# Layer 3 of a four-layer network on one core: the window permutation moves from PE's reads and ACT's eviction to PE's PSUM writes

## The chip, the cores and the metric

The kernel runs on one core of a Trainium2 chip. The metric is the device time of one execution in microseconds (us). One execution was also taken by the hardware profiler; the tables and lines below are from it. PE is TensorE, DVE is VectorE, ACT is ScalarE, POOL is GpSimd, and SP is the engine that issues the DMAs.

## The reference, cut to what matters

Eight images of 32 channels and 256 x 256 pixels pass four layers, each of the form `x = x + layer(groupnorm(x))`. Layer 0 is a depthwise 5 x 5 convolution behind a 1 x 1 one, layer 1 an "adder" convolution (a sum of absolute differences over 32 x 9 taps for each of 32 outputs), layer 2 a 3 x 3 convolution. Layer 3, which the change touches, works on windows of 8 x 8 pixels:

```python
wins = xh.reshape(B, H // WS, WS, W // WS, WS, C).transpose(0, 1, 3, 2, 4, 5).reshape(-1, WS, WS, C)
y = _layernorm(wins, pn_g, pn_b)
a = _fastkan(...)                 # along the rows of a window
d = _fastkan(...)                 # along its columns
e = _fastkan(y.reshape(b, WS * WS, C), ...)
z = a + d + e
z = _fastkan(z.reshape(b, WS * WS, C), ...)
out = z + wins
```

A `_fastkan` is a layer norm, eight Gaussian bases `exp(-((ln - grid) / denom)**2)`, a product with weights over features and bases, and the product of `silu(x)` with a second weight matrix. There are four of them; below they are KAN 0 to 3, and KAN 3 is the last, whose output is added to its window's input.

## The kernel before, in words

**Tiles.** A tile of layer 3 (a "unit") is [128, 2048] fp32: four blocks of 32 channels on the partitions, eight rows of 256 pixels along the free axis. An image has `U` = 8 units, so there are 64 in all. Within 512 columns (two rows) pixels lie in image order, `(r v j)`: row, window, column in the window. KAN 2 and KAN 3 work in the order `(r j v)`, the window index innermost. Whoever reads image order in window order steps 8 elements (32 bytes) from one element to the next.

**Products.** `mm16` (line 587) does one 32-wide channel product of a whole unit: 16 fp32 matmuls of 32 x 32 x 512, four row blocks by four column blocks of PE's array, into the four banks of the PSUM tile psB (`psB` is a single buffer, [128, 4, 512]). The trace has two MATMUL rows for each fp32 matmul, so an `mm16` is 32 rows, all at line 593. Who called it is seen from the tiles: `bas,tl` and `arena,tl` are bases, centrings and sums with constant weights, `si,tl` the SiLU terms, `arena,wt` the centred input of `front`, `si,wt` the residual of KAN 3.

**Layer 3, unit by unit.** `front` (line 1278) loads the unit's input x3 and centres it over the channels with `cenf`, reading it through `windows` (line 1200), so that PSUM holds window order; ACT copies it out (line 1219), squares it (line 1224), PE sums the squares (line 1232), and ACT makes the inverse roots. `middle` scales it (line 1272, on DVE). `kan(n, t)` (line 1334) scales its input and makes eight bases: a square on ACT (line 1368) or on DVE (line 1374), the exponential on ACT (line 1381), and for each basis one `mm16` accumulating into psB (`main`, line 1354). Then the SiLU term (line 1434) and what is in `more`: for KAN 2 the outputs of KANs 0 and 1, for KAN 3 the residual, x3 read once more through `windows` (line 1432). ACT evicts psB to SBUF: KANs 0 to 2 in order (line 1447), KAN 3 back to image order (line 1449):

```python
nc.scalar.activation(
    sb(o).rearrange("p (i v j) -> p i j v", i=8, j=8),
    psB.rearrange("p s (r j v) -> p (s r) j v", r=2, j=8),
    AF.Identity,
    bias=obias,
)
```

It reads PSUM in order and writes SBUF 8 elements apart. SP then stores the unit to the output (line 1471). For the last image, where layer 1 no longer runs, `variance` and `scale` work in two halves on psA instead of psB (`parts`, line 1204).

**Layer 1.** DVE makes a distance of 128 x 4128 bf16 (line 977; some halves on ACT, line 979) and PE sums it with eight matmuls, a "gather" (`gather`, line 990, trace line 999), into psA. There are three buffers for distances (`NDV`, kind "dv").

**What sets the order.** All of it is ordered ahead by a list planner (`Plan`, line 105). Each task has an engine, a planned duration (`mm16` 1.03 us, an eviction 1.97, a gather 0.53) and a rank; `Plan.run` plays the four queues SP, PE, DVE and ACT against each other with these durations and a latency from one engine to the next (`LAT`, line 110), and each engine's instructions are then written out in the order that results. Distances and gathers are "fillers" (`Plan.fill`, line 346, and `Pass.on_pe`, line 404) that go in where an engine has no ranked task. A square may go to DVE (`square.other`) if DVE is free when ACT isn't. Ranks are the number of the image plus a share: layer 3 of image b has b + 1.1 to b + 1.98, so the highest is below 8.1 + 0.88.

Of the kernel before, what the change touches and what calls it, by code (L numbers as in the profile page):

```python
# [20 lines left out]
C = 32  # L21
# [7 lines left out]
FS = F // S  # L29
GRID = 8  # L30
# [35 lines left out]

BASE = 16 * (W + 2) // 2
ROOM = [("bas", 3 * BASE, BASE), ("si", 3 * F, F), ("rs", F // 2, F // 4), ("xr", F // 2, F // 2), ("sb", 10 * F, 0)]
URGENT = 2
IDLE = 8.0  # L70
NDV = 3
# [33 lines left out]
class Plan:  # L105
# [1 line left out]

    LAT = {"PE": 0.15, "DVE": 0.12, "ACT": 0.25, "SP": 2.0}  # L110

    def __init__(self, room):
        self.tasks, self.passes = [], []

        self.free, self.places, at = {}, {"psA": [0], "psB": [0], "psV": [0, 1], "dv": list(range(NDV))}, 0
        for kind, n, size in room:
            if size:
                self.places[kind] = list(range(n // size))
            else:
                self.free[kind] = [(at, n)]  # L120
                at += n
        self.first_pass = 0
        self.sets = []

    def add(self, eng, us, fn, r=(), w=(), rank=0.0, after=(), table=None, spare=0, kb=0, acc=()):
# [102 lines left out]
    def run(self):  # L228
# [23 lines left out]
        while left or any(not p.done for p in self.passes):  # L252
            moved = True
            while moved:
                moved = False
                for e in engines:
                    if busy[e] > now + 1e-9:
                        continue
                    best = self.fill(e, True)
                    if best is None:  # L260
                        for t in ready[e]:
                            if best is not None and (t.rank, t.n) >= (best.rank, best.n):
                                continue
                            if t.table in (LN_EXP, SILU) and t.stretch != self.head:
                                continue
                            if t.eng != e and not all(p.done for p in self.passes[self.first_pass :]):
                                continue
                            if t.gate and not t.gate(self):
                                continue
                            if self.fits(t.need, t.spare):  # L270
                                best = t
                        if best is not None:
                            ready[best.eng].remove(best)
                            if best.other:
                                ready[best.other[0]].remove(best)
                                if best.eng != e:
                                    self.sets[best.stretch][1] -= 1
                                    best.eng, best.us, best.fn, best.table = (*best.other, None)
                    if best is None:
                        best = self.fill(e, False)  # L280
                    if best is None:
                        continue
                    t = best
                    self.take(t.need)
                    us = t.us
                    t.load = None
                    if t.table in (LN_EXP, SILU):
                        self.sets[self.head][1] -= 1
                        self.head += not self.sets[self.head][1]
                        if table != t.table:  # L290
                            t.load = table = t.table
                            us += 1.4
                    t.start = now
                    order.append(t)
                    if e == "SP":
                        busy[e] = now + us
                        mover = max(mover, now + us) + t.kb / 210.0
                        t.end = mover
                    else:
                        busy[e] = t.end = now + us  # L300
                        if e == "ACT" and t.n is not None:
                            self.idle = t.end
                    heapq.heappush(events, (busy[e], 1, count, None))
                    heapq.heappush(events, (t.end, 2, count, t))
                    count += 1
                    moved = True
            if not events:
                break
            now = self.now = events[0][0]
            while events and events[0][0] <= now + 1e-9:  # L310
                _, what, _, t = heapq.heappop(events)
                if what == 0:
                    arrive(t)
                elif what == 2:
                    t.over = True
                    left -= t.n is not None
                    for b in t.bufs:
                        b.left -= 1
                        if not b.left:
                            self.drop(b)  # L320
                    for d in t.outs:
                        d.wait -= 1
                        lat = 0.0 if d.eng == t.eng and t.eng != "SP" else self.LAT[t.eng]
                        d.ready = max(d.ready, t.end + lat)
                        if not d.wait:
                            if d.ready <= now:
                                arrive(d)
                            else:
                                push(d)
                    if t.n is None:  # L330
                        t.ended(t)
# [10 lines left out]

    def slack(self, p):
        return p.b == 0 or self.now - self.idle > IDLE

    def fill(self, e, urgent):

# [17 lines left out]
class Pass:  # L365
# [38 lines left out]
    def on_pe(self, plan, urgent):  # L404
# [3 lines left out]

        late = (9 - len(self.sums)) * 9 < 9 * 9 - self.left or not (self.terms or self.rest or self.queue)
        if self.sums and len(self.queue) < URGENT and (late or not (urgent or self.queue)):  # L410
            t, us, bufs, n = self.sums.pop(0), 0.53, [], 1
            fn = lambda: self.parts.gather(self, None, None, t)
        elif self.queue and (len(self.queue) >= URGENT or not urgent):
            o, t, d = self.queue.pop(0)
            us, bufs, n = 0.53, [d], 1
            fn = lambda: self.parts.gather(self, d, o, t)
        elif not self.added and self.residual.over and (self.left < 20 or not urgent):
            us, bufs, n = 1.75, [], 0
            fn = lambda: self.parts.residual(self)
            self.added = True  # L420
        else:
            return None
# [14 lines left out]
def kernel(  # L437
# [146 lines left out]
        for q in range(NQ):  # L584
            fn(slice(q * C, (q + 1) * C), q)

    def mm16(o, weights, src, start, stop, first=0):

        for j in range(S):
            for i in range(first, min(4, first + o.shape[1])):  # L590
                rows = slice(i * C, (i + 1) * C)
                w_ = weights(i, j) if callable(weights) else weights[rows]
                nc.tensor.matmul(o[j * C : (j + 1) * C, i - first, :], w_, src(rows, i, j), start=start, stop=stop)  # L593

    def spans(t):
        return lambda rows, i, j: t[rows, j * FS : (j + 1) * FS]
# [573 lines left out]
    def stage3(b, norm, x3buf, rank, span):  # L1170
# [5 lines left out]
        def fold():  # L1176
# [20 lines left out]
        stat = {(k, t): (Buf("psV"), Buf("rs")) for t in range(-2, U + 2) for k in "ABC"}  # L1197
        turn = lambda t: r((t + 2) / (U + 4))
        st = [dict() for _ in range(U)]
        windows = lambda t: (  # L1200
            lambda rows, i, j: t[rows, j * FS : (j + 1) * FS].rearrange("c (r v w) -> c r w v", r=2, w=8)
        )

        def parts():

            if b < nb - 1:
# [71 lines left out]
        def front(t, after, rk):  # L1278
# [2 lines left out]
                "SP", 0.5, lambda: nc.sync.dma_start(sb(xt), im["x3"][t]),  # L1281
                r=[x3buf[t]], w=[xt], rank=rk, after=[*norm.done.writers, *after], spare=SPARE + F, kb=1024,
            )
            cen = lambda o, i: mm16(o, cenf, windows(sb(xt)), True, True, i)
            st[t]["c4"] = variance(4, ("A", t - 1), cen, cb, rk, [xt, sm["cenf"], sm["c3"]], xt)

        def middle(t):
# [46 lines left out]
        def kan(n, t, at, rk):  # L1334
# [13 lines left out]
                        nc.sync.dma_start(dst, to_f(d)[g])  # L1348

            acc = Buf("psB")  # L1350
            bases = []
            exps = []

            def main(k):
                mains.append(plan.add(
                    "PE", 1.03,
                    lambda bas=bases[k]: mm16(psB, tl[:, WK + 9 * n + k, :], spans(sb(bas)), k == 0, False),
                    r=[bases[k]], w=[acc], rank=rk,
                ))
                if k == 0:  # L1360
# [65 lines left out]
            if n == 3:  # L1426
# [2 lines left out]
                    "SP", 0.5, lambda a=a: nc.sync.dma_start(sb(a), im["x3"][t]),  # L1429
                    r=[x3buf[t]], w=[a], rank=rk, after=exps[4:5], spare=F, kb=1024,  # L1430
                )
                more.append((a, resf, lambda rows, i, j, a=a: windows(sb(a))(rows, i, j)))
            plan.add(
                "PE", 1.03, lambda: mm16(psB, tl[:, WK + 9 * n + GRID, :], src, False, not more),
                r=[si], w=[acc], rank=rk,
            )
            for m, (a, wm, s_) in enumerate(more):
# [5 lines left out]
            obias = b4 if n == 3 else col(KCOL + 2 * n + 1)  # L1443

            def evict():
                if n < 3:
                    nc.scalar.activation(sb(o), psB.rearrange("p s f -> p (s f)"), AF.Identity, bias=obias)  # L1447
                else:
                    nc.scalar.activation(  # L1449
                        sb(o).rearrange("p (i v j) -> p i j v", i=8, j=8),  # L1450
                        psB.rearrange("p s (r j v) -> p (s r) j v", r=2, j=8),
                        AF.Identity,
                        bias=obias,
                    )

            st[t][f"end{n}"] = plan.add(
                "ACT", 1.97, evict, r=[acc] + ([sm["c3"]] if n == 3 else []), w=[o], rank=rk - 0.001
# [216 lines left out]
```

## Time and profile before

| | us |
|---|---|
| median of 3 runs | 15973.13 |
| lowest, highest | 15972.10, 15999.17 |
| the profiled execution | 15969.78 |
| its span, first to last instruction | 15967.3 |

| engine | busy us | share of the span |
|---|---|---|
| DVE | 13454.6 | 84% |
| PE | 12928.0 | 81% |
| ACT | 12386.4 | 78% |
| PE weight loads (overlap PE) | 4325.8 | 27% |

The span has three parts: up to 2.4 ms the first image goes through layers 0 and 1; up to 14.6 ms layer 1 of one image runs beside layer 3 of the image before and the other layers between them; from 14.6 ms the last image's layers 2 and 3 run alone.

How to read a group of the profile: line, engine, operation, output <- inputs, shapes, x count | busy us, mean ns of one | idle us of the engine just before them, and what ended it. In a timeline a row is start, duration, engine, line, operation and count of merged instructions, with the engine's idle time before it in brackets. In a table of stretches, each engine has its busy us and, in brackets, its instructions; the last three numbers are the granted clock, the DMA share and GB/s.

### The profile page before, as it was taken

The page shows a single profiled execution, that of the slowest core. Times are in us where ns is not written, and L with a number is a line of the kernel's source. Part 1 is how long each engine was busy: PE and PEld are TensorE (multiplying, and loading weights), DVE is VectorE, ACT ScalarE, POOL GpSimd, SP SyncE. Part 2 cuts the span into 40 slices and gives each one's busy share as a digit, 9 for nine tenths or more (in the row PEclk, how much of TensorE's full clock was granted, in tenths as well). Part 3 has the DMA queues.
Part 4 walks back from the last instruction along what each step waited for, and adds up shares of the span by engine and source line. Part 5 has one row for each costly group of instructions (what it writes and reads, how often), then busy time and mean ns, then how long its engine had stood idle before and what let it go on. Part 6 is the DMA issues. An engine that isn't in the chain of part 4 may idle for free. (4 is left out here: it accounts for less than half of the span.)

```text
span 15967.3 us, 560619 instructions
## 1 busy us (share of the span) xinstructions
PE 12928.0 (81%) x260296; PEld 4325.8 (27%) x260296; DVE 13454.6 (84%) x12544; ACT 12386.4 (78%) x6843; POOL 16.7 (0%) x25
## 2 busy tenths in 40 slices
PE   5889887987887888788887888788878888877666
PEld 4333322222332222232222222222222222222222
DVE  2889889898878889888999988999898989897465
ACT  0899749678658766866888987899779987997687
POOL 0000000000000000000000000000000000000000
PEclk8989899999999999899999999899999999998777
DMA  4332446445445444643554454444544454444554
GB/s 117 78 96 54 105 113 169 109 107 153 130 101 152 126 112 120 166 106 105 152 132 123 126 134 122 122 123 127 127 126 126 126 122 138 116 132 114 144 154 130
DMA packets 1192870, 1970.85 MB, mean 123 GB/s; under 512 B 362752, under 2 KB 878848, under 8 KB 1092224
## 3 DMA queue, kind: packets, MB, share of 16 engines
q1 hardware_dynamic: 1190528, 1934.98, 46.1%
q8 instruction: 2036, 33.36, 0.9%
q14 instruction: 306, 2.51, 0.1%
HBM read 1162.83 MB, written 771.75 MB: 121 GB/s over the span
## 5 line engine op out<-in xcount | busy, mean ns | idle before, releaser
L977 DVE TENSOR_SCALAR dv<-qh,w1q 128x4128 bf16<-128x4128 bf16 (+1 forms) x8831 | 10521.9, 1248 | 1376.3 <-PE psA L999 1319.3
L999 PE MATMUL psA<-dv,sel_b 128*32 128x512 bf16 x71240 | 5434.0, 405 | 1339.6 <-DVE dv L977 1054.2
L999 PEld LDWEIGHTS <-sel_b 128*32 128x32 bf16 x82944 | 2053.9, 97 | 6792.6 <-issue 5786.5
L1368 ACT ACTIVATE bas<-arena,kb 128x2048 f32<-128x2048 f32 x1386 | 2762.3, 1993 | 408.3 <-DVE arena L1272 262.9
L1381 ACT ACTIVATE bas<-bas 128x2048 f32<-128x2048 f32 x1386 | 2653.1, 1914 | 39.0
L979 ACT ACTIVATE dv<-qh,w1n 128x2064 bf16<-128x2064 bf16 x827 | 1628.6, 2009 | 1126.8 <-PE psA L999 1035.3
L593 PE MATMUL psB<-bas,tl 32*32 32x512 f32 x48416 | 1955.5, 652 | 491.1 <-ACT bas L1381 247.6
L873 PE MATMUL psB<-arena,wt 32*32 32x512 f32 (+1 forms) x51040 | 1848.5, 607 | 99.5 <-issue 61.4
L593 PE MATMUL psB<-arena,tl 32*32 32x512 f32 x22496 | 909.4, 621 | 161.7 <-ACT si L1449 46.1
L593 PEld LDWEIGHTS psB<-bas,tl 32*32 32x32 f32 x48416 | 535.2, 107 | 1384.3 <-ACT bas L1381 518.8
L873 PEld LDWEIGHTS psB<-arena,wt 32*32 32x32 f32 x51040 | 651.2, 104 | 778.1 <-issue 607.1
L1368 ACT ACTIVATE arena<-arena,kb 128x2048 f32<-128x2048 f32 x410 | 816.1, 1991 | 0.0
L1381 ACT ACTIVATE arena<-arena 128x2048 f32<-128x2048 f32 x410 | 785.0, 1915 | 12.3
L624 DVE BATCH_NORM_STATS2 tiny<-arena 128x6 f32<-128x512 f32 x768 | 473.5, 679 | 351.8 <-ACT arena L906 246.0
L999 PE MATMUL psA<-qh,sel_b 128*32 128x512 bf16 x9216 | 672.2, 393 | 92.3 <-DMA qh<-q 77.9
L1447 ACT ACTIVATE si<-psB,cols_sb 128x2048 f32<-128x2048 f32 x192 | 377.4, 1966 | 453.3 <-PE psB L593 369.9
L1272 DVE TENSOR_TENSOR arena<-psB,arena 128x2048 f32<-128x2048 f32 x280 | 640.5, 2287 | 86.2 <-PE psB L1264 79.2
L593 PE MATMUL psB<-si,tl 32*32 32x512 f32 x14080 | 630.6, 624 | 48.8 <-ACT si L1447 19.5
L1129 PE MATMUL psB<-arena,tl 32*32 32x512 f32 (+3 forms) x16384 | 626.6, 608 | 14.7 <-issue 14.4
L1224 ACT ACTIVATE arena<-arena 128x2048 f32<-128x2048 f32 x320 | 612.7, 1915 | 15.7 <-DMA x<-arena 5.8
L1264 PE MATMUL psB<-rs,tl 32*32 32x512 f32 x8960 | 338.9, 630 | 222.5 <-DVE arena L1272 128.2
L906 ACT ACTIVATE arena<-psB,cc 128x2048 f32<-128x2048 f32 x64 | 125.7, 1964 | 493.2 <-PE psB L894 493.2
(151 smaller groups left out, 7686.6 us busy)
## 6 DMA issues: line engine op xcount, KB each, us to landing
arena<-x SPq DMA_DIRECT2D x128, 1024.0 KB
arena<-y SPq DMA_DIRECT2D x128, 1024.0 KB
si<-sy SPq DMA_DIRECT2D x512, 256.0 KB
arena<-in_x_dram SPq DMA_DIRECT2D x240, 384.0 KB
arena<-in_x_dram SPq DMA_DIRECT2D x256, 256.0 KB
x<-arena SPq DMA_DIRECT2D x256, 256.0 KB
xr<-x SPq DMA_DIRECT2D x512, 128.0 KB
x<-xr SPq DMA_DIRECT2D x512, 128.0 KB
```

Of the source, the lines that this page charges most:

```text
L593: nc.tensor.matmul(o[j * C : (j + 1) * C, i - first, :], w_, src(rows, i, j), start=start, stop=stop)
L624: nc.vector.bn_stats(self.stats[:, at + i, :], a[:, i * 512 : (i + 1) * 512])
L873: nc.tensor.matmul(o[:, lo - 2 * j : hi - 2 * j, c0:c1], wt[rows, t, :], d[rows, lo + dy + 2 : hi + dy + 2, c0 + dx : c1 + dx], start=firs ...
L977: nc.vector.tensor_scalar(dst, src, w1q[:, at : at + 1], 0.0, ALU.subtract, ALU.max)
L979: nc.scalar.activation(dst, src, AF.Relu, bias=w1n[:, at : at + 1])
L999: nc.tensor.matmul(psA[j * C : (j + 1) * C, i, :], sel_b[:, n, :], src[:, at : at + 2, t % 3 : t % 3 + W], **flags,)
L1129: nc.tensor.matmul(o[:, lo - 2 * j : hi - 2 * j, c0:c1], (wc if t == 4 else tl[:, W2T + t, :])[rows], d[rows, lo + dy + 1 : hi + dy + 1, c ...
L1224: plan.add("ACT", 1.9, lambda: nc.scalar.activation(sb(sq), sb(c), AF.Square), r=[c], w=[sq], rank=rk)
L1272: lambda ps=ps, at=at: nc.vector.tensor_tensor(sb(c)[:, at], ps().rearrange("p s f -> p (s f)"), sb(c)[:, at], ALU.mult),
L1368: lambda k=k, bas=bas: nc.scalar.activation(sb(bas), sb(rb), AF.Square, bias=kb[:, n, k : k + 1]),
L1381: lambda k=k, bas=bas, square=square: nc.scalar.activation(sb(bas), sb(bas), AF.Exp, scale=-1.0, bias=0.0 if square.eng == "ACT" else kbsq ...
L1447: nc.scalar.activation(sb(o), psB.rearrange("p s f -> p (s f)"), AF.Identity, bias=obias)
```

## The change

Two views are added and handed to `mm16`, which can now write its PSUM rows in another order than it reads. In `front` the centring reads x3 in order and writes it to PSUM in window order (`to_window`: 32 elements apart). In KAN 3 all ten products (eight bases, SiLU term, residual) go to PSUM in image order (`by_window`: the first nine read window order and write 8 elements apart; the residual reads and writes in order). KAN 3's eviction then is that of the other KANs. `windows` goes.

The planner also changes: the latencies, the gather's planned duration (0.53 to 0.49), 0.05 us planned for PE at each switch between gathers and ranked work, and a branch (`AHEAD`) that lets a filler go ahead of a PE task whose rank is more than 9 above the number of the image that layer 1 is at.

```diff
+AHEAD = 9.0
...
-    LAT = {"PE": 0.15, "DVE": 0.12, "ACT": 0.25, "SP": 2.0}
+    LAT = {"PE": 0.2, "DVE": 0.15, "ACT": 0.3, "SP": 2.0}
...
-        self.first_pass = 0
+        self.first_pass, self.filling = 0, False
...
-                        if best is not None:
+                        if best is not None and e == "PE" and best.rank > self.image() + AHEAD:
+                            piece = self.fill(e, False)
+                            if piece is not None:
+                                best = piece
+                        if best is not None and best.n is not None:
                             ready[best.eng].remove(best)
...
                     t.load = None
+                    if e == "PE":
+                        us += 0.05 * ((t.n is None) != self.filling)
+                        self.filling = t.n is None
...
+    def image(self):
+        return next((p.b for p in self.passes[self.first_pass :] if not p.done), len(self.passes))
...
-            t, us, bufs, n = self.sums.pop(0), 0.53, [], 1
+            t, us, bufs, n = self.sums.pop(0), 0.49, [], 1
...
-            us, bufs, n = 0.53, [d], 1
+            us, bufs, n = 0.49, [d], 1
...
-    def mm16(o, weights, src, start, stop, first=0):
+    def by_window(o):
+
+        return o.rearrange("p (r v j) -> p r j v", r=2, j=8)
+
+    def to_window(o):
+
+        return o.rearrange("p (r j v) -> p r v j", r=2, j=8)
+
+    def mm16(o, weights, src, start, stop, first=0, view=lambda o: o):
...
-                nc.tensor.matmul(o[j * C : (j + 1) * C, i - first, :], w_, src(rows, i, j), start=start, stop=stop)
+                nc.tensor.matmul(view(o[j * C : (j + 1) * C, i - first, :]), w_, src(rows, i, j), start=start, stop=stop)
...
-        windows = lambda t: (
-            lambda rows, i, j: t[rows, j * FS : (j + 1) * FS].rearrange("c (r v w) -> c r w v", r=2, w=8)
-        )
...
-            cen = lambda o, i: mm16(o, cenf, windows(sb(xt)), True, True, i)
+            cen = lambda o, i: mm16(o, cenf, spans(sb(xt)), True, True, i, to_window)
...
+            view = by_window if n == 3 else lambda o: o
...
-                    lambda bas=bases[k]: mm16(psB, tl[:, WK + 9 * n + k, :], spans(sb(bas)), k == 0, False),
+                    lambda bas=bases[k]: mm16(psB, tl[:, WK + 9 * n + k, :], spans(sb(bas)), k == 0, False, view=view),
...
-                more.append((a, resf, lambda rows, i, j, a=a: windows(sb(a))(rows, i, j)))
+                more.append((a, resf, lambda rows, i, j, a=a: sb(a)[rows, j * FS : (j + 1) * FS]))
             plan.add(
-                "PE", 1.03, lambda: mm16(psB, tl[:, WK + 9 * n + GRID, :], src, False, not more),
+                "PE", 1.03, lambda: mm16(psB, tl[:, WK + 9 * n + GRID, :], src, False, not more, view=view),
...
             def evict():
-                if n < 3:
-                    nc.scalar.activation(sb(o), psB.rearrange("p s f -> p (s f)"), AF.Identity, bias=obias)
-                else:
-                    nc.scalar.activation(
-                        sb(o).rearrange("p (i v j) -> p i j v", i=8, j=8),
-                        psB.rearrange("p s (r j v) -> p (s r) j v", r=2, j=8),
-                        AF.Identity,
-                        bias=obias,
-                    )
+                nc.scalar.activation(sb(o), psB.rearrange("p s f -> p (s f)"), AF.Identity, bias=obias)
```

## The prediction

> **What bounds the kernel now.** I read the busy times first, then the same shares by stretches of the span, because the stages have different limits.
>
> ```profile
> PE 12928.0 (81%) x260296; PEld 4325.8 (27%) x260296; DVE 13454.6 (84%) x12544; ACT 12386.4 (78%) x6843; POOL 16.7 (0%) x25
> ...
> 8000.00:14000.00 6000.00, 4890.53 (x92432) 1534.18 (x92421) 5436.81 (x4614) 5166.62 (x2865) 8.56 (x7) 0.93 0.48 127
> 15098.00:15868.00 770.00, 519.44 (x9576) 185.16 (x9576) 477.78 (x241) 636.81 (x386) 0.00 (x0) 0.77 0.54 147
> ```
>
> Over the whole span no engine is above 84%. In the middle (8 to 14 ms: one image's adder passes beside the KAN units of the image before), VectorE (DVE) is busy 5436.8 of 6000 us, 91%, ScalarE (ACT) 86%, TensorE (PE) 82%. There the three take turns at being late: the waits put 1319 us of DVE's idle time to PE's gather line 999 and 1054 us of PE's to DVE's line 977. In the tail (from 14.6 ms, the last image's eight units with no adder left) ACT is the fullest, 637 of 770 us, 83%. The chain that ended last lies in the tail alone, and its largest single line is the `mm16` helper, L593, with 1.3% of the span.
>
> The groups, shapes kept apart, price what is touched:
>
> ```profile
> L593 PE MATMUL psB<-bas,tl 32*32 32x512 f32 x48416 | 1955.5, 652 | 491.1 <-ACT bas L1381 247.6 <-ACT arena L1219 64.1 <-ACT si L1447 63.9
> ...
> L1447 ACT ACTIVATE si<-psB,cols_sb 128x2048 f32<-128x2048 f32 x192 | 377.4, 1966 | 453.3 <-PE psB L593 369.9 <-PE psA L999 70.0 <-DMA arena<-in_x_dram 9.1
> ...
> L1449 ACT ACTIVATE si<-psB,cc 128x2048 f32<-128x2048 f32 x64 | 262.0, 4094 | 107.5 <-PE psB L593 107.4
> ...
> L593 PE MATMUL psB<-si,wt 32*32 32x512 f32 x2048 | 153.8, 1085 | 4.2 <-issue 4.0
> ...
> L593 PE MATMUL psB<-arena,wt 32*32 32x512 f32 x1792 | 117.6, 1086 | 10.4 <-ACT arena L1219 6.1 <-DVE cc L1190 3.2 <-ACT si L1447 0.9
> ```
>
> The last KAN's eviction (L1449) moves the same 128x2048 as the other KANs' (L1447) and takes 4094 ns against 1966: it writes SBUF 32 bytes apart. The two products that read windows, the residual (`si,wt`) and the centred input (`arena,wt`), take 1085 ns a row against some 620 for rows that read in order. One `mm16` is 32 rows (16 fp32 products, two rows each). How one eviction sits in time, in the middle:
>
> ```profile
> 10583.23 2.50 DVE L977 TENSOR_SCALAR dv<-qh,w1q 128x4128 bf16<-128x4128 bf16 x2 [1.40 <-PE psA L999]
> ...
> 10583.54 2.10 PE L593 MATMUL psB<-si,wt 32*32 32x512 f32 x32
> ...
> 10585.57 0.62 PE L999 MATMUL psA<-dv,sel_b 128*32 128x512 bf16 x8
> ...
> 10585.82 4.15 ACT L1449 ACTIVATE si<-psB,cc 128x2048 f32<-128x2048 f32 x1 [1.63 <-PE psB L593]
> 10586.01 1.03 PE L1232 MATMUL psV<-arena,tl 128*32 128x512 f32 x8
> 10586.24 6.33 DVE L977 TENSOR_SCALAR dv<-qh,w1q 128x4128 bf16<-128x4128 bf16 x5 [0.51 <-PE psA L999]
> ```
>
> The residual occupies PE for 2.03 us before the next gather; DVE, out of buffers, idles 1.40 and 0.51 us around it, and ACT idles 1.63 us for the residual before its 4.15 us eviction. PE waits little here, as gathers fill it; over all units it idles about 83 us behind L1449.
>
> **The change, part by part.**
>
> *Eviction.* 64 units (8 images of 8) x (4.094 - 1.966) = 136 us off ACT. Both of its sides are in order now, as in L1447, so I count this as nearly certain.
>
> *Residual and centred reads.* An `mm16` that reads windows spans 2.10 us from first start to last end, one in order 1.15. Residual: it reads and writes in order now, as psB holds image order; 64 x 0.95 = 61 us of PE. Centred input (reads in order, writes permuted): 56 units on psB x 0.95 = 53 us; the last image's 8 units go in 16 halves on psA, where the rows fall from 1089 ns to about 750: 16 x 0.34 = 5 us. Together 119 us of PE, 58 of them only if the permuted write is free.
>
> *Permuted writes.* They replace the read in the 64 centred products and are new in nine of each last KAN (eight bases and the SiLU term): 64 x 9 = 576 `mm16`. They land 32 bytes apart (centred input: 128), and no row of this trace writes PSUM so at length, so I bound it. It can't gain, since the writes it replaces are in order. From above, the nearest rows are the reads 32 bytes apart: +0.95 us each, 547 us of PE, and then the centred products' 58 us aren't saved either. I take zero, for this reason:
>
> ```profile
> 2615.61 1.04 PE L999 MATMUL psA<-qh,sel_b 128*32 128x512 bf16 x16
> ...
> 2616.48 0.61 PE L999 MATMUL psA<-dv,sel_b 128*32 128x512 bf16 x8
> ...
> 2617.02 1.14 PE L593 MATMUL psB<-bas,tl 32*32 32x512 f32 x32
> ...
> 2617.90 1.47 PE L593 MATMUL psB<-si,tl 32*32 32x512 f32 x32
> ```
>
> At full clock 16 bf16 gathers take 1.04 us and 8 take 0.61, so eight more cost 0.43; they put 2 x 512 columns into each column tile, 0.215 us per 512 columns of a bank. The fp32 `mm16` from 2617.02 to the next at 2617.90 takes 0.88 us for 2 x 512 columns into each of four banks that fill side by side: 0.44 us per 512. So fp32 products write a bank at half the rate that the gathers show it to take. What the strided accesses here cost is a factor of two (the read 2.10 for 1.15 us, ACT's write 4.09 for 1.97); a write that is halved from the rate of the gathers still keeps up with fp32.
>
> [...]
>
> *The planner's constants.* The order of every queue (PE, DVE, ACT, SP) is made by the plan, so latencies of 0.2/0.15/0.3, a gather at 0.49 in place of 0.53, and 0.05 at each switch between gathers and other PE work reorder everything, the DMA issues among it. The same work is issued (no DMA or wait is added), though the plan also chooses whether a square or a distance runs on ACT or on DVE, so busy time can move between the two. 82944 gather rows are 10368 gathers: -0.04 each is 415 us less planned on PE, and the switches put up to 0.05 x 10368 = 518 back. The isolated gather of the trace (0.61) and the next one's 0.43 lie on both sides of either figure, so no row says which order is better. I take zero, with 100 us either way: some 8% of the 1319 us that DVE waits for gathers. The `AHEAD` branch asks for a rank over the image's number plus 9; the highest rank is below 8.1 + 0.88 = 8.98, and the lowest image is 0, so it never runs and costs nothing.
>
> *What passes on.* Per unit the residual, then the eviction, then the next user of the single psB form one chain; 0.95 + 2.13 = 3.08 us leave it. In the tail I count all of it: 8 x 3.08 = 25 us. In the middle the fullest engine is DVE. I took DVE's busy share in slices of 2 us around the 54 residuals between 2.4 and 14.6 ms: it falls from about 0.92 to 0.80, 0.82, 0.61, 0.92, 0.83, 0.82, which is 0.72 x 2 = 1.4 us lost per unit, while around the other KANs' evictions it stays at 0.92. So if DVE binds, 56 x 1.4 = 80 us come back; if ACT binds, 56 x 3.08 = 172. With 91% against 86% both bind by turns; I take the middle, 126. Around the centred products DVE shows no lasting dip (0.86 to 1.00), so I count their 58 us at nothing: gathers and waiting distances hide them, and uncovered they'd be 58 more. SP's store of the output (L1471) is issued 2 to 3 us earlier and nothing waits on that. Sum: 126 + 25 = 151 us off the profiled execution's 15969.8 us (its span 15967.3 and 2.5 around it), 15819. The median of the runs shown is 15973.1, 3 us more and less than a measurement tells; I say **15820**. What is late next is ACT's square and exp of the bases (2.0 + 1.9 us each).
>
> **Rivals.**
>
> *The strided write costs what the strided read costs: slower.* +547 us of PE. Cover: where ACT makes a base in 3.9 us, PE's base (1.15) and three gathers (some 1.5) leave over 1 us, and 0.95 would hide; where bases stand ready (the first three or four of a unit) or DVE has no buffer, nothing hides it. At half, +274, less the 151 of eviction and residual: +123, **16090**; if all passes, 547 - 151 gives 16370. It decides from where the loss on 576 products at half weight eats the 151 us: 151 / (0.5 x 576) = 0.52 us per `mm16`. For: reads and ACT's writes both lose a factor of two at this stride. Against: the gathers' rate.
>
> *Hidden or eaten.* DVE binds, the 80 us are all that returns, and the new order costs 50 to 100: within 0.2% (32 us), about **15960**. For: 91% DVE, and a DVE wait is as much its own order as PE's.
>
> *A worse order alone.* The direct gain is real and the order costs 200 or more: **16020**. Against: the eviction and the strided reads were planned at 1.97 and 1.03, which they now meet, so the plan fits better than before.
>
> **The numbers.** Forecast, 15690 to 15930: 0.70. Strided write: 0.17. Hidden: 0.08. Worse order: 0.05. A measurement here tells about 0.2% from no change, so faster 0.70, same 0.08, slower 0.22. Range for 8 in 10: below, 151 + 100 (order) + 58 (centred products uncovered) gives 15660; above, it goes into the strided write's case to 16100, leaving out half of that case (0.09) and, at both ends, up to 0.1 elsewhere.
>
> **What would show it.** The 64 evictions that use `cc` fall from 4.09 to 1.97 us; `si,wt` and `arena,wt` rows fall to 610 to 650 ns and their `mm16` to 1.15 us; the mean of the rows of bases (`bas,tl`) stays at some 650. If the write costs, 18432 of the rows from bases and SiLU stand near 1085 and PE's busy time grows by some 500 us. DVE's share around the last KAN's eviction should rise by 1.4 us per unit; ACT's busy time falls by 136 us, give or take what the plan moves to or from DVE. I am wrong if the strided write loses over 0.52 us, or if PE's waits for DVE and ACT grow elsewhere by more than 100 us through the order.

## The result and the profile after

The changed kernel takes 15815.5 us (median, 15803.4 to 15820.4) against 15973.7 for the kernel before: ratio 0.9895, 95% interval 0.988 to 0.991, 158 us less. In a later session, beside experiment 11, it took 15790.9 where the kernel before took 15978.9: ratio 0.988 (0.9865 to 0.9895), 188 us less. The predicted time was 15820. In the changed kernel `mm16` is line 612, the gather 1018, the distance 996, the centred eviction 1234 and every KAN's eviction 1462.

The page's busy times:

```profile
PE 12814.9 (81%) x260296; PEld 4330.4 (27%) x260296; DVE 13427.1 (85%) x12536; ACT 12262.5 (78%) x6849; POOL 33.1 (0%) x25
```

The middle stretch and 770 us of the tail (columns as in the section on the profile before):

```profile
8000.00:14000.00 6000.00, 4883.39 (x93994) 1566.43 (x93994) 5529.40 (x4715) 5199.70 (x2919) 11.63 (x7) 0.94 0.49 130
14940.00:15710.00 770.00, 527.00 (x9706) 179.48 (x9701) 482.90 (x245) 631.80 (x389) 0.00 (x0) 0.76 0.55 151
```

Against before PE is busy 113 us less and ACT 124; DVE's share of the middle goes from 91% to 92%, and counted from 2.4 to 14.4 ms its idle time falls from 1331 to 1237 us. The tail looks as before, with ACT the fullest.

The groups by shape, in the changed kernel (the last row belongs to the last image's halves; in the kernel before it had a mean of 1089 ns):

```profile
L612 PE MATMUL psB<-bas,tl 32*32 32x512 f32 x48544 | 1953.2, 653 | 438.8 <-ACT bas L1397 240.1 <-DVE arena L1287 59.5 <-ACT arena L1234 52.6
...
L1462 ACT ACTIVATE si<-psB,cc 128x2048 f32<-128x2048 f32 x64 | 125.7, 1964 | 82.8 <-PE psB L612 77.5 <-DMA xr<-x 5.1
...
L612 PE MATMUL psB<-si,wt 32*32 32x512 f32 x2048 | 89.2, 645 | 2.6 <-issue 2.5
...
L612 PE MATMUL psB<-arena,wt 32*32 32x512 f32 x1792 | 70.9, 665 | 9.7 <-ACT arena L1234 4.7 <-ACT si L1462 1.8 <-DVE arena L1287 1.6
...
L612 PE MATMUL psA<-arena,wt 32*32 32x512 f32 x256 | 23.4, 769 | 13.7 <-ACT arena L1234 13.7
```

KAN 3's eviction (`si<-psB,cc`) falls from 4094 to 1964 ns. The residual's rows (`si,wt`) fall from 1085 to 645 ns and the centred input's from 1086 to 665, though the latter now write 128 bytes apart. The bases' rows, of which KAN 3's now write 32 bytes apart, stay at 653 ns (652 before).

The unit shown in the prediction, in the changed kernel's timeline:

```profile
10493.45 8.66 DVE L996 TENSOR_SCALAR dv<-qh,w1q 128x4128 bf16<-128x4128 bf16 x7 [0.32 <-PE psA L1018]
...
10495.38 1.14 PE L612 MATMUL psB<-si,wt 32*32 32x512 f32 x32
...
10496.45 0.62 PE L1018 MATMUL psA<-dv,sel_b 128*32 128x512 bf16 x8
...
10496.70 1.98 ACT L1462 ACTIVATE si<-psB,cc 128x2048 f32<-128x2048 f32 x1 [0.66 <-PE psB L612]
```

The residual holds PE for 1.07 us instead of 2.03 before the next gather follows, ACT idles 0.66 us before the eviction instead of 1.63, the eviction takes 1.98 us instead of 4.15, and DVE's run of distances isn't broken any more.

### The profile page after: what moved, and what is told of

Its sections match the earlier page's. It is cut to its first block, busy times and chain, and to the rows that moved or that the text cites. A ratio compares the mean times of both kernels' runs of the same rounds, so it can differ in the third digit from the quotient of the medians.

```text
span 15808.7 us, 560681 instructions
## 1 busy us (share of the span) xinstructions
PE 12814.9 (81%) x260296; PEld 4330.4 (27%) x260296; DVE 13427.1 (85%) x12536; ACT 12262.5 (78%) x6849; POOL 33.1 (0%) x25
## 4 chain that ended last, share of the span: by engine, by line
PE 22%; ACT 20%; DVE 6%; issue 6%; DMA 1%; SPq 0%; DVEq 0%; ACTq 0%
PE psB L612 9%; PE psA L1018 7%; ACT bas L1384 5%; ACT bas L1397 4%; DVE dv L996 3%; ACT arena L1384 2%; PE psB L1148 2%; ACT arena L1397 2%; ACT arena L1234 2%; PE psB L892 1%; ACT si L1462 1%; ACT arena L1239 1%; DVE arena L1287 1%; PE psV L1247 1%; DVE arena L1390 1%
## 5 line engine op out<-in xcount | busy, mean ns | idle before, releaser
L1148 PE MATMUL psB<-arena,tl 32*32 32x510 f32 (+3 forms) x16384 | 626.6, 610 | 19.9 <-issue 19.8
L1234 ACT ACTIVATE arena<-psB 128x2048 f32<-128x2048 f32 x224 | 418.9, 1870 | 127.1 <-PE psB L612 126.5
```

Of the source, the lines that this page charges most:

```text
L1148: nc.tensor.matmul(o[:, lo - 2 * j : hi - 2 * j, c0:c1], (wc if t == 4 else tl[:, W2T + t, :])[rows], d[rows, lo + dy + 1 : hi + dy + 1, c ...
L1234: lambda ps=ps, at=at: nc.scalar.activation(sb(c)[:, at], ps().rearrange("p s f -> p (s f)"), func, bias=shift),
```

## The experiments

Each kernel is compared with the kernel before on the same chip; ratios carry their 95% interval.

**1. All views, the order of before.** The change with the planner's old constants:

```diff
-    LAT = {"PE": 0.2, "DVE": 0.15, "ACT": 0.3, "SP": 2.0}
+    LAT = {"PE": 0.15, "DVE": 0.12, "ACT": 0.25, "SP": 2.0}
...
-                        us += 0.05 * ((t.n is None) != self.filling)
+                        us += 0.0 * ((t.n is None) != self.filling)
...
-            t, us, bufs, n = self.sums.pop(0), 0.49, [], 1
+            t, us, bufs, n = self.sums.pop(0), 0.53, [], 1
...
-            us, bufs, n = 0.49, [d], 1
+            us, bufs, n = 0.53, [d], 1
```

> The views of the change with the planner's constants of before, so that every queue keeps the order of before. My theory (the time comes from KAN 3's eviction and the reads, 3.08 us per unit; the new order gives nothing): 151 us less than before, 15820, ratio 0.9905, the same as the whole change. Rival 'order' (the new order gives most of the 158 us, since DVE binds and hides the rest): 80 us less or below, 15890 or above, ratio 0.995 to 1.0.

Measured: 15790.9 against 15976.6, ratio 0.9888 (0.9874 to 0.9901), 186 us less. The views give all of the gain; the rival that the order gives it falls. They give some 35 us more than the 151 that I had counted, whose source experiments 4 and 6 look for. Since each queue has the order of before here, the two traces can be laid side by side: KAN 3's evictions start 6 us earlier in the first unit, 80 in the 32nd and 181 in the last. The gain comes evenly, 2.8 us per unit. The page's busy times:

```profile
PE 12795.4 (81%) x260296; PEld 4293.2 (27%) x260296; DVE 13443.0 (85%) x12544; ACT 12252.9 (78%) x6843; POOL 17.3 (0%) x25
```

PE has lost 133 us, ACT 134 and DVE 12, so what DVE does is unchanged; it waits some 171 us less. DVE and ACT run the same instructions in the same order as before, though the `AHEAD` branch is in this kernel: it does nothing, as forecast.

**2. The planner's constants, the views of before.**

```diff
-            cen = lambda o, i: mm16(o, cenf, spans(sb(xt)), True, True, i, to_window)
+            cen = lambda o, i: mm16(o, cenf, windows(sb(xt)), True, True, i)
...
-            view = by_window if n == 3 else lambda o: o
+            view = lambda o: o
...
```

(and the residual's read and the eviction as before)

> The planner's constants of the change with the views of before: another order, and the 4.09 us evictions and 1.09 us read rows kept. My theory: within 100 us of before either way, 15970 with a ratio of 0.994 to 1.006. Rival 'order': 80 to 160 us less, 15810 to 15890, ratio 0.990 to 0.995.

Measured: 16019.7, ratio 1.0029 (1.0019 to 1.0039): 43 us more. The new order alone is no gain; on the old views it is a small loss, within the 100 us that I had set.

**3. The reads, with the strided eviction kept.** The centred input and the residual are read in order and written by `to_window`; KAN 3's sums stay in window order.

```diff
-            view = by_window if n == 3 else lambda o: o
+            view = lambda o: o
...
-                    "PE", 1.03, lambda wm=wm, s_=s_, m=m: mm16(psB, wm, s_, False, m == len(more) - 1),
+                    "PE", 1.03, lambda wm=wm, s_=s_, m=m: mm16(
+                        psB, wm, s_, False, m == len(more) - 1, view=to_window if n == 3 else lambda o: o
+                    ),
```

> Constants and order of before; the centred input and the residual read in order and write PSUM permuted, but KAN 3's sums stay in window order and its eviction stays the 4.09 us one. It takes 119 us off PE and nothing off ACT. My theory: the residual's 0.95 us is on the chain (61 us), the centred product's isn't (0 to 58): 61 us less, 15910, ratio 0.996. Rival 'DVE hides PE': under 25 us, ratio above 0.9985. If the permuted write costs as much as the read, nothing changes at all.

Measured: 15909.1, ratio 0.9961 (0.9948 to 0.9973), 67 us less. PE's busy time falls by 110 us (12928.0 to 12818.5), so 61% of what leaves PE leaves the time, though PE is the least full of the three in the middle. "DVE hides PE" falls.

**4. The centred input alone.** Experiment 3 with the residual read through `windows` as before.

> Constants and order of before; of the views only the centred input's. 58 us less on PE. My theory: hidden by gathers and waiting distances, 0 to 20 us less, ratio 0.9987 to 1.0. Rival 'every PE us counts': 58 us less, ratio 0.9964.

Measured: 15937.6, ratio 0.9977 (0.9968 to 0.9986), 39 us less (22 to 51), of 58 off PE. My expectation of 0 to 20 falls, and "every us counts" does too. It also changes how experiment 3 reads: if the two add up, the residual's read gave some 28 us (67 less 39, give or take 25) and not the 61 that I had counted, so that 67 lies near my 61 in part by luck: two errors that cancel.

ACT evicts the centred product. Its rows, before and then in this kernel (behind the bar: busy, mean, and ACT's idle time before it):

```profile
L1219 ACT ACTIVATE arena<-psB,cc 128x2048 f32<-128x2048 f32 x56 | 110.3, 1970 | 85.3 <-PE psB L593 85.3
```

```profile
L1237 ACT ACTIVATE arena<-psB,cc 128x2048 f32<-128x2048 f32 x56 | 110.0, 1964 | 51.8 <-PE psB L612 51.6
```

ACT waited 85.3 us for the centred product and now waits 51.8, 34 us less. But this trace can't show where the 39 us went: its execution was the slowest of the eleven, 15967.5 us (the fastest took 15918.6), only 2 us under the profiled one of before. ACT's idle time in all is the same in both, 3581 us, as ACT waits longer elsewhere. A better pair is experiment 6 below and experiment 1, which differ by the centred product alone and whose profiled spans, one execution each, differ by 35 us (15819.3 and 15784.2). The same row in the two:

```profile
L1237 ACT ACTIVATE arena<-psB,cc 128x2048 f32<-128x2048 f32 x56 | 110.4, 1971 | 87.0 <-PE psB L612 86.8
```

```profile
L1234 ACT ACTIVATE arena<-psB,cc 128x2048 f32<-128x2048 f32 x56 | 110.0, 1964 | 52.4 <-PE psB L612 52.3
```

There the wait falls by 35 us, ACT's idle time in all by 33 and DVE's by 29. So ACT's wait for this product falls by the size of the gain. That the time comes back through ACT and not through DVE is argued and not shown, since both idle less when the whole gets shorter.

**5. What a stride in PSUM costs at bf16's rate.** Two kernels with the views and the order of before, whose gathers write their columns in another order: each column alone, 32 bytes from the next one written ("lone elements"), or two neighbours together ("pairs"). Each was run once:

```diff
-                        psA[j * C : (j + 1) * C, i, :],
+                        psA[j * C : (j + 1) * C, i, :].rearrange("p (v j) -> p j v", j=8),              # lone elements
+                        psA[j * C : (j + 1) * C, i, :].rearrange("p (v j t) -> p j v t", j=4, t=2),     # pairs
```

> Before, with the bf16 gathers writing each bank's 512 columns 32 bytes apart; it changes what is computed (layer 1's sums land on permuted pixels), the order stays. It asks whether a write apart costs nothing in PSUM at all, or is only covered at fp32's rate. My theory (a bank takes lone elements at half its best rate, which fp32 doesn't reach): eight gather rows cost 0.86 us more in place of 0.43, a lone gather 1.05 in place of 0.61; the time grows by thousands of us, some 17500 to 20500. Rival (PSUM doesn't mind strides): rows and time as before, 15970. [...]

> Before, with the bf16 gathers writing pairs of neighbouring columns, the pairs 32 bytes apart; it changes what is computed in the same way. [...]

Measured, lone elements: 18267 us. The rows, in the groups and in a timeline at full clock:

```profile
L999 PE MATMUL psA<-dv,sel_b 128*32 128x512 bf16 x71240 | 8848.2, 635 | 559.6 <-DVE dv L977 390.1 <-ACT dv L979 89.2 <-ACT xr L1046 60.4
```

```profile
2608.53 1.04 PE L999 MATMUL psA<-dv,sel_b 128*32 128x512 bf16 x8
2610.56 1.90 PE L999 MATMUL psA<-dv,sel_b 128*32 128x512 bf16 x16
...
2637.51 2.76 PE L999 MATMUL psA<-dv,sel_b 128*32 128x512 bf16 x24
```

One, two and three gathers take 1.04, 1.90 and 2.76 us: 0.86 for each further one, where before each cost 0.43. A stride in PSUM isn't free: for these gathers it halves the rate at which a bank takes columns, from 0.215 to 0.43 us per 512. The fp32 products need 0.44 us per 512 (the prediction's 0.88 us for 2 x 512), so a bank at that rate would still keep up with them. "PSUM doesn't mind strides" falls, and my theory's 0.86 holds. The gathers differ from the fp32 products in type and shape as well as in rate, so that the rate decides is the reading that fits; no run changes it alone.

Pairs: 16598 us. Four rows of the timeline, all at full clock:

```profile
2622.90 0.61 PE L999 MATMUL psA<-dv,sel_b 128*32 128x512 bf16 x8
...
2625.11 1.48 PE L999 MATMUL psA<-dv,sel_b 128*32 128x512 bf16 x24
...
2629.14 2.75 PE L999 MATMUL psA<-dv,sel_b 128*32 128x512 bf16 x24
...
2638.71 1.04 PE L999 MATMUL psA<-dv,sel_b 128*32 128x512 bf16 x8
```

Gathers of both kinds stand side by side: some as in order (0.61 us alone, 1.48 for three), some as with lone elements (1.04 and 2.75). At full clock 70% of the gathers that stand alone take 0.61 us and 30% take 1.04. Which ones they are is seen by counting the 72 gathers of distances in each of the 128 passes in their order, eight for each of the nine taps. The rows of the three taps whose read begins at the second column (an odd bf16 element) have a median of 627 ns in the trace at full clock, and all of them are over 550; those of the other six have a median of 379, and none is over 550. So pairs are as good as order where the read begins at an even element, and as bad as lone elements where it begins at an odd one. Two neighbours together are thus enough here for the rate of order (379 ns a row), if the read starts even; why an odd start loses it, no run shows.

**6. KAN 3's views alone**, the centred input read through `windows` as before.

```diff
-            cen = lambda o, i: mm16(o, cenf, spans(sb(xt)), True, True, i, to_window)
+            cen = lambda o, i: mm16(o, cenf, windows(sb(xt)), True, True, i)
```

> The views of KAN 3 alone (sums written permuted, residual read in order, eviction in order), the centred input read through windows as before; constants and order of before. My theory: the chain of 3.08 us per unit, 151 us less, 15825, ratio 0.9906. If it adds up with the centred product alone (39 less) to all views (186 less): 147. Rival 'DVE hides': 80 or less, ratio above 0.995.

Measured: 15820.9 against 15985.9, ratio 0.9897 (0.9881 to 0.9914), 165 us less (137 to 190). This is the chain that I had priced at 151. With experiment 4's 39 it makes 204, against 185 and 186 for all views; the gap is inside the intervals. In the profiled execution KAN 3's eviction is 126 us early in the 56th unit, the last before the last image, and 147.9 us are gone at the end: 126 in the middle and 22 in the tail, where the prediction had 126 and 25.

**7. All views without the permuted writes of KAN 3's sums.**

```diff
-            view = by_window if n == 3 else lambda o: o
+            view = lambda o: o
```

> All views and the order of before, but KAN 3's nine sums are written in order; the sums then lie in window order beside the residual in image order, so it changes what is computed. Against all views it takes away only the 576 permuted writes. My theory: they cost nothing, the same time, 15790 give or take 15, ratio 0.988 to 0.990. Rival (each costs something under the 10% that row means would hide): up to 0.05 us per product at the weight of the residual, 15 us less.

Measured: 15795.5, ratio 0.9883 (0.9869 to 0.9898), against 0.9888 and 0.9881 for all views. The 576 permuted products cost nothing that shows. The times alone, good to some 20 us, could hide the rival's 15, but the rows settle it: at full clock they have a median of 588 ns in KAN 3 and 588 in the other KANs, in the kernel before, in all views and in this one alike, and one whole product of KAN 3's nine spans 1.14 us in all three.

**8 to 11. The planner's constants on the new views**, in halves, and the whole change beside all views alone.

> The change with the latencies of before: of the planner's constants only the gather's 0.49 and the 0.05 per switch. All views alone gave 186 us less, the whole change 158. Theory 'any order is as good within some 50 us': 15760 to 15850, and this run's and the next one's shifts against all views alone needn't add up to the whole change's. Rival 'one constant is the cost': either this one stands with the whole change (15815) and the next with all views alone (15790), or the other way round.

> The change with the gather at 0.53 and nothing per switch: of the planner's constants only the latencies. Theories and numbers as for the run before it: 15760 to 15850 under 'any order', 15815 or 15790 under 'one constant'.

> The whole change once more, beside all views alone on the same chip. My reading of the runs so far: the planner's new constants cost 20 to 45 us, so this one is at ratio 0.9895 and all views alone at 0.9885. Rival: the two are alike, and the difference was the chip.

> All views alone once more, beside the whole change on the same chip: 0.9885, 20 to 45 us under the whole change; alike under the rival.

| kernel | us | ratio (interval) |
|---|---|---|
| gather and switch only | 15807.6 | 0.9891 (0.9875 to 0.9908) |
| latencies only | 15836.7 | 0.9908 (0.9893 to 0.9923) |
| the whole change | 15790.9 | 0.9880 (0.9865 to 0.9895) |
| all views alone | 15793.8 | 0.9881 (0.9866 to 0.9896) |

The whole change and all views alone are alike, so the 28 us that seemed to lie between them came from comparing two sessions: my reading falls and the rival holds. What differs between the sessions, the chip or something else, no run separates. The halves (14 and 43 us above all views, in the same session) don't add up to the whole's -3, which speaks for "any order is as good within some 50 us" and against "one constant is the cost", though the halves' intervals touch the others'. In the trace the new order ends layer 1 of the second image some 60 us later than before and makes it up in the images that follow. No kernel here clearly beats the changed one.

One thing that I overlooked goes along with these differences: the mean granted clock of an execution, as a share of TensorE's full speed. Among executions of one kernel in one session, each 0.001 more of it goes with some 5.5 us less (a line fitted to 84 executions). Its mean was 0.9238 in experiment 1 and 0.9235 in experiment 6, where the kernel before beside them had 0.9214 and 0.9203, and 0.9184 in experiment 2. By this estimate some 13 of the 186 us, 18 of the 165 and 16 of the 43 go with the clock. It was 0.962 in the one execution with experiment 5's lone elements, so it isn't alike for all kernels; whether these views move it, no run shows.

## Why the prediction was right, point by point

*Bound and chain: right in the main.* KAN 3's views alone give 165 us (137 to 190), 2.6 us per unit, of the 3.08 that leave the chain of residual, eviction and next use of psB. DVE's share in slices of 2 us from the residual's start was 0.82, 0.61, 0.92, 0.83, 0.82 and is 0.88, 0.91, 0.97, 0.97, 0.94 with all views and the old order: 1.3 us per unit, where 1.4 was forecast. How the 165 divide between the two parts is less sure: experiments 3 and 4 together leave some 28 us for the residual's read.

*Eviction and reads: right in size.* 64 x (4.094 - 1.964) = 136 us of ACT; with the order held ACT's busy time falls by 134 (12386.4 to 12252.9). PE's falls by 133 there and by 113 in the whole change; the forecast was 119. The psA halves came to 769 ns a row, forecast 750.

*Permuted writes at nothing: right, and the reason given fits.* It was the step with the most riding on it. Experiment 7 shows the zero. Experiment 5 shows the factor of two for the bf16 gathers that write lone elements (0.86 us for eight rows more in place of 0.43), and fp32's rate (0.44 us per 512 columns) would cover the 0.43 that this leaves. The fp32 products themselves show no loss (588 ns a row both ways). The rival that the strided write costs what the strided read costs would have added 547 us to PE.

*The order at nothing, give or take 100: right.* 43 us more on the old views (some 16 of them with the clock), nothing that shows on the new ones. That the plan fits the new durations better may be why it costs less there; this was argued, not shown.

*What passes on: the step that failed is* "Around the centred products DVE shows no lasting dip (0.86 to 1.00), so I count their 58 us at nothing". Alone they give 39 us (22 to 51), and between all views and KAN 3's alone some 20. I asked only the fullest engine. ACT's row for that eviction stood in the same list with 85.3 us of idle time before it, all put to the product, and some 34 of them go; that this wait, of an engine that is 86% full, is what brought the time back fits the numbers but isn't shown. With it, and with the clock, all views give 186 and not 151. That the first measurement of the change, 158, lies so near to 151 is in part chance; in the later session it is 188.

*The middle taken between 80 and 172: right by choice, not by proof.* In experiment 6's profiled execution 126 us come back in the middle, just the 126 taken. That is luck as much as insight: the choice between "DVE binds" and "ACT binds" was a mean of two bounds, neither end holds, and that execution's 148 us in all lie under the 165 of the medians.

## What to carry to other kernels

If experiment 5 is read rightly, put a permutation where the stream is already slower than the memory's rate out of order: here fp32 products fill a PSUM bank at half of the rate that bf16 shows (0.44 us per 512 columns against 0.215), and PE writes apart at no cost that shows (588 ns a row both ways), while PE's strided reads and ACT's strided write each took about twice the time (2.10 us against 1.15, 4.09 against 1.97). And when no engine is full, ask of a saving which engines wait for it, and not the fullest alone: the 85 us of idle time before the consumer's row were a sign that the saving would not come to nothing. They were no price, as 34 of them went.

## What the runs showed of the hardware that I had not expected

A bf16 product that writes pairs of neighbouring fp32 columns, the pairs 32 bytes apart, runs as in order (379 ns a row at full clock) if its read begins at an even element, and near the lone elements' rate (627 ns, lone elements 633) if it begins at an odd one, although the pairs in PSUM lie at the same addresses. With writes in order the odd start costs nothing that matters (381 ns against 379). And the same pair of kernels stood at ratio 0.9895 (0.988 to 0.991) in one session and at 0.9880 (0.9865 to 0.9895) in another, some 25 us apart in the changed kernel's time, as much as between the halves of a plan: here I take differences of this size only between kernels that were run in one session.
